# Two moves in a four-layer graph network kernel: layer 0's factors ahead of x, and the last block's third product around its last sums

## The chip, the cores and the metric

The kernel runs on one core of one Trainium2 chip, all in float32. The metric is the device time of one execution in microseconds (us). Three runs of the kernel before took 2646.83, 2647.34 and 2647.69 us; the median, 2647.34 us, is what a changed kernel is held against.

## The reference

The input x holds 128 graphs of 64 nodes with 512 features. Each of four layers normalizes x, takes the positive part, runs a graph layer on it and adds the result to x:

```python
h = jnp.maximum(_layernorm(x, axis=-1), 0.0)
x = x + _L0_gnn_ref(h, adj, nodemask, L0_gnn_Wqk, L0_gnn_Wv)
```

Layer 0 computes, for each node, `w = -q . (adj @ (k * mask))` up to a scale, with `q = h @ Wq`, `k = h @ Wk`, and multiplies `softmax(w) * (h @ Wv)`. Because q and k only meet in a product, the kernel works with one folded matrix, Wq times the transpose of Wk, which it computes itself at the start. Layers 1 and 2 are attention layers with the adjacency as weight or mask; layer 3 is a graph attention layer with three powers of the transition matrix:

```python
for k in range(Wk.shape[0]):
    H = H + Xk @ Wk[k] + bk[k]
    Xk = jnp.einsum('bij,bjd->bid', transition, Xk)
return jax.nn.relu(H)
```

In the kernel this is reordered: y1 = h Wk1 and y2 = h Wk2 are formed first, then y1 + A y2, then y0 + A (y1 + A y2), where A is the transition matrix and y0 = h Wk0 plus the sum of the three bias rows.

## The kernel before

The 8192 tokens are cut into 32 blocks of 256 tokens (four graphs), each two tiles of 128. Layers 0 and 1 run for two blocks at a time, in the order 0, 0, 1, 1 (`steps`, L915); then layer 2 runs over all blocks, then layer 3. The result of layer 1 and of layer 2 is kept in device memory between the passes.

A product of a block with a 512 x 512 weight (class `Product`, L228) is computed with seven half-size products in place of eight. `sums` (L209) makes the four sums of the block's quarters S1 to S4 on POOL (GpSimd); `formed` (L85) makes the four sums of the weight's quarters. Each of the seven is two matmuls of 128 x 256 columns (L256 or L249). The products use two PSUM tiles of one bank each: ab holds the halves a and b, dc holds d and c. Product 1 starts a, 6 starts b, 5 starts c, 4 is d; later 2 is added to a, 7 to b and 3 to c. Between them `keep_ab` (L281) copies a to p1 and forms u2 = b + p1, and `keep_dc` (L288) copies c to p5. The four quarters of the result are a, c + u2, d + u3 and u3 + p5, with u3 = b + p1 after product 7.

`neighbour_sums` (L390) multiplies a block by the adjacency or transition weights of its four graphs: four matmuls of 64 x 64 x 512 (L397), written to `pa` in layer 0 and to `po` in layer 3.

**The start.** At L136 the program issues the load of block 0's x, of its adjacency and of the mask on SP's queue. Then come the two factors of layer 0 (L139): q on ACT's queue and k on SP's, each in four pieces of 256 KB. The value weight of layer 0 (L143) and small rows follow. At L947 to L952 the order is: `prepare(0)`, the normalization of block 0 (`norm`, L164: statistics L169 and L170, ve L172, reciprocal root on POOL L174, nmr L176, h on ACT L184); `transpose_weight` of q (L416, sixteen transposes and four copies back into the same tile, two on DVE and two on ACT); `turned(0)`, the transposes of h (L195); `transpose_weight` of k, two of whose PSUM tiles come from the pool of the products; `setup0` (L450), which computes the fold in sixteen matmuls (L440), copies each piece out on ACT and DVE (L444, L445) and forms the four sums of the folded weight on DVE; and the sums of the value weight on POOL (L952). Layer 1's set-up (`setup1`, L459) loads that layer's weights and bias rows and does nine dot products on DVE (L478); the first of them, d, needs only the two bias rows.

**The end.** For a block b, `layer3_tail` (L851) runs y0's products 1, 6, 5 and 4, then the denominators (den, L861) and the second sums (`po2`), whose result updates y1 on DVE (L872), then products 2, 7 and 3 (`late`) and their results with the bias row bs (L881 to L886). `layer3_end` (L889) runs the last sums (`po3`), scales them by r, adds y0, takes the positive part, adds x (L904) and stores. Of the last block, tile 0 is scaled and added in one DVE operation (L896), while tile 1 goes through ACT (L900) and POOL (L903); the two tiles are stored apart (L908).

**What sets the order.** The program text gives the dependencies and a priority. A scheduler of the framework puts the instructions into each engine's queue when the kernel is built, by times that it models, and adds the waits. `tc.issue_after(i)` holds an instruction behind instruction i in that order. [...]

Of the kernel before, what the change touches and what calls it, by code (L numbers as in the profile page):

```python
# [8 lines left out]
FP = mybir.dt.float32  # L9
# [4 lines left out]
P = 128  # L14
# [11 lines left out]
def kernel(ctx: ExitStack, tc: tile.TileContext, a: dict, out: bass.AP):  # L26
# [101 lines left out]
    def factor(ap, which: str, layer: int, queue):  # L128
# [4 lines left out]
            queue.dma_start(w[:, k, :], ap[k * P : (k + 1) * P, :])  # L133
        return w

    first = load_x(0, x_d[rows(0), :], 0), load_adjT(0, 0)  # L136
    mcol = const.tile([P, n_tok // P], FP, tag="mcol", name="mcol")
    nc.sync.dma_start(mcol, a["maskcol"])
    f0 = [  # L139
        factor(a["L0_Wqk"][:, i * D : (i + 1) * D], c, 0, queue)  # L140
        for i, (c, queue) in enumerate((("q", nc.scalar), ("k", nc.sync)))
    ]
    w0v = fetched("L0_Wv", 1, nc.sync)  # L143
    b2q, b2k = (column(n) for n in ("L2_bq", "L2_bk"))
    b1v = row("L1_bv")
# [270 lines left out]
    def transpose_weight(w, name: str, places=((ps_mm, "mm"),) * K, on_scalar=(1, 3)):  # L416

        pts = [
            pool.tile([P, K, P], FP, tag=tag, name=f"tw_{name}_{m}")
            for m, (pool, tag) in enumerate(places)  # L420
        ]
        for k in range(K):
            for m, pt in enumerate(pts):
                nc.tensor.transpose(pt[:, k, :], w[:, k, m * P : (m + 1) * P], ident)
        for m, pt in enumerate(pts):
            flat = pt.rearrange("p k i -> p (k i)")
            if m in on_scalar:
                nc.scalar.copy(w[:, m, :], flat)
            else:
                nc.vector.tensor_copy(w[:, m, :], flat)  # L430

    elsewhere = ((ps_tr, "tr"), (ps_sc, "sc")) * 2

    def folded(aT, bT, layer: int, place: int, amid=lambda: None):

        m = slot(place, f"fold{layer}")
        for i in range(K):
            pm = ps_mm.tile([P, D], FP, tag="mm", name=f"pf_{layer}_{i}")
            for k in range(K):
                nc.tensor.matmul(  # L440
                    pm, aT[:, k, i * P : (i + 1) * P], bT[:, k, :],
                    start=(k == 0), stop=(k == K - 1),
                )
            nc.scalar.copy(m[:, quarters[i // 2][0], i % 2, :], pm[:, :F])  # L444
            nc.vector.tensor_copy(m[:, quarters[i // 2][1], i % 2, :], pm[:, F:])  # L445
            if not i:
                amid()
        return m

    def setup0():  # L450
        m = folded(*f0, 0, 0)
        formed(m, nc.vector)

        msc = const.tile([P, n_tok // P], FP, tag="msc", name="msc")
        with tc.issue_after(behind_norm[0][1].ins):
            nc.vector.tensor_scalar(msc, mcol, -(float(D) ** -0.5), None, ALU.mult)
        return m, msc
# [393 lines left out]
    def layer3_tail(b: int, al, ops, y):  # L851


        p = Product(f"y0_{b}")
        p.first(ops, w3[0])
        p.second(ops, w3[0])
        yield
        den = [ps_tr.tile([P, 1], FP, tag="tr", name=f"den3_{b}_{t}") for t in range(TT)]
        for t in range(TT):
            for g in range(2):  # L860
                nc.tensor.matmul(  # L861
                    den[t][half[g ^ t]], al[half[g], t, :], ones_bd[half[g], g * N : g * N + 1],
                    start=True, stop=True,
                )
        po = [ps_sc.tile([P, D], FP, tag="sc", name=f"po2_{b}_{t}") for t in range(TT)]
        parts = neighbour_sums(po, al, [y[:, 1, t, :] for t in range(TT)])
        r = small.tile([P, TT], FP, tag="r1", name=f"r3_{b}")
        for t in range(TT):
            nc.vector.tensor_scalar(r[:, t : t + 1], den[t], 1e-12, None, ALU.add)
        nc.vector.reciprocal(r, r)  # L870
        for t, to, at in parts:
            nc.vector.scalar_tensor_tensor(  # L872
                y[to, 0, t, :], po[t][at], r[at, t : t + 1], y[to, 0, t, :], ALU.mult, ALU.add
            )
        bs = made3[2]
        y0 = big.tile([P, TT, D], FP, tag="v", name=f"y0_{b}")
        nc.gpsimd.tensor_tensor(p.u2, p.u2, bs[:, F:], ALU.add)
        nc.gpsimd.tensor_tensor(p.p5, p.p5, bs[:, F:], ALU.add)
        yield
        p.late(ops, w3[0])  # L880
        nc.vector.tensor_tensor(y0[:, 0, :F], p.a, bs[:, :F], ALU.add)  # L881
        nc.vector.tensor_tensor(p.u3, p.b, p.p1, ALU.add)  # L882
        nc.vector.tensor_tensor(y0[:, 1, :F], p.d, p.u3, ALU.add)
        nc.gpsimd.tensor_tensor(y0[:, 1, F:], p.u3, p.p5, ALU.add)
        kept = nc.vector.tensor_tensor(y0[:, 0, F:], p.c, p.u2, ALU.add)
        nc.gpsimd.tensor_tensor(y0[:, 1, :F], y0[:, 1, :F], bs[:, :F], ALU.add)  # L886
        yield r, y0, kept

    def layer3_end(b: int, x, al, y, r, y0):  # L889

        po = [ps_sc.tile([P, D], FP, tag="sc", name=f"po3_{b}_{t}") for t in range(TT)]
        tz = [med.tile([P, D], FP, tag="pT", name=f"tz_{b}_{t}", bufs=3) for t in range(TT)]
        to, last = tokens(out[rows(b), :]), b + 1 == n_blk
        for t, out_at, at in neighbour_sums(po, al, [y[:, 0, t, :] for t in range(TT)]):
            if last and not t:
                nc.vector.scalar_tensor_tensor(  # L896
                    tz[t], po[t], r[:, t : t + 1], y0[:, t, :], ALU.mult, ALU.add
                )
            else:
                nc.scalar.activation(tz[t][out_at], po[t][at], AF.Copy, scale=r[at, t : t + 1])  # L900
        for t in range(TT):
            if not last or t:
                nc.gpsimd.tensor_tensor(tz[t], tz[t], y0[:, t, :], ALU.add)  # L903
            nc.vector.scalar_tensor_tensor(  # L904
                x[:, t, :], tz[t], 0.0, x[:, t, :], ALU.max, ALU.add
            )
            if last:
                nc.sync.dma_start(to[:, t], x[:, t])  # L908
        if not last:
            nc.sync.dma_start(to, x)  # L910


    x1 = [tc.dram_tile([T, D], FP, name=f"x1_{b}") for b in range(n_blk)]
# [11 lines left out]
    def turned(i: int):  # L925
        layer, b = steps[i]
        normed[i] = normed[i], transposed(normed[i], f"{layer}_{b}")
# [16 lines left out]
        if b < n_blk:  # L944
            normed2[b] = transposed(normed2[b], f"2_{b}")

    prepare(0)  # L947
    transpose_weight(f0[0], "q0")
    turned(0)
    transpose_weight(f0[1], "k0", ((ps_sc, "sc"),) * 2 + ((ps_mm, "mm"),) * 2)  # L950
    m0, msc = setup0()
    formed(w0v, nc.gpsimd)  # L952
    loaded[1] = load_x(1, x_d[rows(1), :], 0), load_adjT(1, 0)
    setup = setup1()
    next(setup)
# [39 lines left out]
    def layer3_step(b: int, ahead: bool = True):  # L995

        nonlocal normed3
        x, al, ops = made_in.pop(0)  # L1000
        stages = layer3_in(b + 1, *normed3, made_in) if b + 1 < n_blk else iter(())

        def begin():
            nonlocal normed3
            if b + 2 < n_blk and ahead:
                normed3 = layer3_norm(b + 2, x2[b + 2])

        y = layer3_head(b, ops, [
            [begin], [ending.pop()], [lambda: next(stages, None), lambda: next(stages, None)]
        ])  # L1010
# [6 lines left out]
        ending.append(lambda: layer3_end(b, x, al, y, r, y0))  # L1017
        if b + 2 < n_blk:
# [142 lines left out]
```

## Time and profile before

| what | value |
|---|---|
| median of three runs | 2647.34 us |
| the profiled execution's own time | 2645.07 us |
| its span | 2643.3 us |
| TensorE (PE) busy | 2624.6 us, 99% |
| VectorE (DVE) busy | 1695.9 us, 64% |
| GpSimd (POOL) busy | 1292.8 us, 49% |
| ScalarE (ACT) busy | 950.4 us, 36% |
| mean transfer rate over the span | 49 GB/s |
| first transpose on PE | 5.13 us |
| first product of block 0 on PE | 28.79 us |
| last sums on PE start | 2635.43 us |

The profile is of one execution on the core. Times count from the start of the span. In a timeline, a row gives the start, the time from the first to the last instruction of a merged group, the engine, the line in the kernel, the operation, its output and inputs with their sizes, the number of instructions, and in brackets how long the engine stood idle before it and what released it. PEld is the loading of weights into PE, which runs beside the matmuls. SPq and ACTq rows are the issue of transfers. Names in the trace leave out numbers: p_y stands for p1 and p5, u_y for u2 and u3, ab_v and ab_g for the products of layer 0 with the value weight and the fold.

### The profile page before, as it was taken

What the parts mean: (1) busy time and instruction counts of PE and PEld (TensorE: products, weight loads), DVE (VectorE), ACT (ScalarE), POOL (GpSimd) and SP (SyncE); (2) the same over time, 40 slices, a digit from 0 to 9 for tenths busy, and PEclk for the clock granted to TensorE, in tenths of its full rate; (3) what the DMA queues carried; (4) which work ended last, traced back from release to release, by engine and by line L of the source; (5) the groups of instructions that cost most, each with busy time, mean ns of one, the idle gap of its engine ahead of it and who ended that gap; (6) DMA issues with size and microseconds to landing.
All of it is one profiled execution on the core that took longest, in us unless ns stands there. A gap on an engine that the chain in (4) does not pass through costs nothing.

```text
span 2643.3 us, 52749 instructions
## 1 busy us (share of the span) xinstructions
PE 2624.6 (99%) x20752; PEld 2250.6 (85%) x20752; DVE 1695.9 (64%) x4396; ACT 950.4 (36%) x2292; POOL 1292.8 (49%) x1585
## 2 busy tenths in 40 slices
PE   9999999999999999999999999999999999999998
PEld 5888888888888889999999999999877777777776
DVE  5676666666666676556556656656656666666665
ACT  3333343333333343333333333333333333333332
POOL 4443333333433335655655655655565555555554
PEclk9999999999999999999999999999999999999999
DMA  5111111111111122111111111111211111111110
GB/s 179 48 35 35 35 36 37 46 39 43 43 35 35 35 67 79 39 51 40 37 53 38 39 53 37 39 48 42 74 51 52 51 52 52 52 52 51 52 50 32
DMA packets 103200, 129.80 MB, mean 49 GB/s; under 512 B 40870, under 2 KB 50086, under 8 KB 102952
## 3 DMA queue, kind: packets, MB, share of 16 engines
q1 hardware_dynamic: 102376, 125.38, 14.3%
q8 instruction: 163, 2.67, 0.4%
q10 hardware_dynamic: 576, 1.05, 0.1%
q14 instruction: 85, 0.70, 0.1%
HBM read 76.07 MB, written 50.34 MB: 48 GB/s over the span
## 4 chain that ended last, share of the span: by engine, by line
PE 93%; DVE 2%; DMA 2%; POOL 1%; ACT 1%; issue 0%; SPq 0%; ACTq 0%; POOLq 0%; DVEq 0%
PE ab_v L256 12%; PE ab_y L256 11%; PE dc_v L256 9%; PE dc_y L256 8%; PE ab_g L249 4%; PE ab_k L249 4%; PE ab_g L256 4%; PE ab_q L249 4%; PE tr L195 4%; PE ab_o L256 4%; PE dc_g L249 3%; PE dc_g L256 3%; PE po L397 3%; PE dc_k L249 3%; PE dc_q L249 3%; PE dc_o L256 3%
## 5 line engine op out<-in xcount | busy, mean ns | idle before, releaser
L184 ACT ACTIVATE h<-x,nmr,rstd 128x512 f32<-128x512 f32 x256 | 194.4, 806 | 239.8 <-DVE nmr L176 239.8
L174 POOL TENSOR_TENSOR rstd<-ve,neghalf 128x2 f32<-128x2 f32 x128 | 89.6, 700 | 373.8 <-DVE ve L172 373.8
L169 DVE BATCH_NORM_STATS2 stats<-x 128x6 f32<-128x512 f32 x256 | 165.5, 677 | 92.8 <-DMA x<-x 86.7
L256 PE MATMUL ab_y<-L_Wk,hT 128*128 128x256 f32 x768 | 203.9, 388 | 0.1
L256 PE MATMUL ab_v<-L_Wv,hT 128*128 128x256 f32 x768 | 200.8, 384 | 0.4 <-ACT qk L328 0.4
L256 PE MATMUL dc_v<-L_Wv,S 128*128 128x256 f32 x768 | 197.3, 380 | 0.0
L256 PE MATMUL ab_y<-L_Wk,S 128*128 128x256 f32 x768 | 197.2, 379 | 0.0
L256 PE MATMUL ab_v<-L_Wv,S 128*128 128x256 f32 x768 | 197.2, 379 | 0.0
L256 PE MATMUL dc_y<-L_Wk,S 128*128 128x256 f32 x768 | 193.8, 381 | 3.2 <-DVE u_y L882 3.1
L256 PEld LDWEIGHTS ab_y<-L_Wk,hT 128*128 128x128 f32 x768 | 137.3, 190 | 67.5 <-issue 25.2
L256 PEld LDWEIGHTS dc_y<-L_Wk,S 128*128 128x128 f32 x768 | 144.8, 190 | 26.6 <-DVE u_y L882 7.0
L256 PEld LDWEIGHTS ab_v<-L_Wv,S 128*128 128x128 f32 x768 | 146.1, 190 | 19.7
L256 PEld LDWEIGHTS ab_y<-L_Wk,S 128*128 128x128 f32 x768 | 146.1, 190 | 19.7
L256 PEld LDWEIGHTS dc_v<-L_Wv,S 128*128 128x128 f32 x768 | 143.6, 190 | 18.7 <-issue 0.8
L903 POOL TENSOR_TENSOR tz<-tz,y 128x512 f32<-128x512 f32 x63 | 91.3, 1450 | 126.0 <-ACT tz L900 125.9
L256 PEld LDWEIGHTS ab_v<-L_Wv,hT 128*128 128x128 f32 x768 | 136.0, 190 | 16.0 <-ACT qk L328 0.7
L195 PE MATMUL tr<-ident,h 128*128 128x128 f32 x1024 | 133.9, 274 | 0.0
L195 PEld LDWEIGHTS tr<-ident,h 128*128 128x128 f32 x1024 | 118.4, 142 | 7.3
L221 POOL TENSOR_TENSOR S<-hT 128x256 f32<-128x256 f32 x128 | 100.4, 784 | 34.0 <-ACT hT L198 33.6
L224 POOL TENSOR_TENSOR S<-hT 128x256 f32<-128x256 f32 x128 | 107.9, 843 | 7.1 <-DVE hT L200 7.1
L904 DVE SCALAR_TENSOR_TENSOR x<-tz,x 128x512 f32<-128x512 f32 x64 | 44.3, 692 | 102.6 <-POOL tz L903 102.6
L311 POOL TENSOR_TENSOR gv<-u_g,p_g 128x256 f32<-128x256 f32 x32 | 23.3, 729 | 173.0 <-DVE u_g L308 173.0
(238 smaller groups left out, 6474.6 us busy)
## 6 DMA issues: line engine op xcount, KB each, us to landing
x<-x SPq DMA_DIRECT2D x128, 512.0 KB, 3.5
x<-in_x_dram SPq DMA_DIRECT2D x32, 512.0 KB, 3.5
out_dram<-x SPq DMA_DIRECT2D x31, 512.0 KB, 2.8
adjT<-in_adjT_dram SPq DMA_DIRECT2D x64, 64.0 KB, 1.9
adjq<-in_adj_dram SPq DMA_DIRECT2D x64, 64.0 KB, 2.3
L_Wk<-in_L_Wk_dram SPq DMA_DIRECT2D x16, 256.0 KB, 5.5
L_Wv<-in_L_Wv_dram SPq DMA_DIRECT2D x12, 256.0 KB, 4.9
q<-in_L_Wqk_dram ACTq DMA_DIRECT2D x4, 256.0 KB, 5.3
```

The lines of the kernel that those rows point to most:

```text
L169: nc.vector.bn_stats(stats[:, t, :], x[:, t, :])
L174: by_rows = nc.gpsimd.tensor_tensor(rstd, ve, neghalf, ALU.pow)
L184: nc.scalar.activation(h, x[:, t, :], AF.Relu, bias=nmr[:, t : t + 1], scale=rstd[:, t : t + 1])
L195: nc.tensor.transpose(pt[:, k, :], h[:, k * P : (k + 1) * P], ident)
L221: nc.gpsimd.tensor_tensor(S1, A21, A22, ALU.add)
L224: behind[0] = nc.gpsimd.tensor_tensor(S3, A11, A21, ALU.subtract)
L249: nc.tensor.matmul(dst[:, m * P : (m + 1) * P], w[:, place, k, m * P : (m + 1) * P], left[:, k, :], start=key not in self.begun, stop=last ...
L256: nc.tensor.matmul(dst, left[:, k, :], w[:, place, k, :], start=key not in self.begun, stop=last and k == 1, skip_group_check=True,)
L311: nc.gpsimd.tensor_tensor(y[:, 1, F:], self.u3, self.p5, ALU.add)
L397: nc.tensor.matmul(ps[t][half[g ^ t]], e[half[g], t, :], us[t][half[g]], start=True, stop=True)
L903: nc.gpsimd.tensor_tensor(tz[t], tz[t], y0[:, t, :], ALU.add)
L904: nc.vector.scalar_tensor_tensor(x[:, t, :], tz[t], 0.0, x[:, t, :], ALU.max, ALU.add)
```

## The change

The factors q and k of layer 0 are issued ahead of block 0's x, adjacency and mask. Both are transposed ahead of all else; k's PSUM tiles all come from the pools of scores and transposes. `transpose_weight` now returns its last copies, and the normalization of block 0 is held behind those of k. The transposes of block 0's h are placed inside the fold, after its first piece. The sums of the value weight go from POOL to DVE, behind the nmr of block 0.

In the last block, products 5 and 4 of y0 follow the second sums; product 7 comes ahead of the last sums, and 3 and 2 behind them. Tile 0's half of y0 starts as the bias row, and a and c are added to its scaled sum at the very end. The other blocks are unchanged.

```diff
+    f0 = [
+        factor(a["L0_Wqk"][:, i * D : (i + 1) * D], c, 0, queue)
+        for i, (c, queue) in enumerate((("q", nc.scalar), ("k", nc.sync)))
+    ]
     first = load_x(0, x_d[rows(0), :], 0), load_adjT(0, 0)
     mcol = const.tile([P, n_tok // P], FP, tag="mcol", name="mcol")
     nc.sync.dma_start(mcol, a["maskcol"])
-    f0 = [
-        factor(a["L0_Wqk"][:, i * D : (i + 1) * D], c, 0, queue)
-        for i, (c, queue) in enumerate((("q", nc.scalar), ("k", nc.sync)))
-    ]
...
     def setup0():
-        m = folded(*f0, 0, 0)
+        m = folded(*f0, 0, 0, lambda: turned(0))
         formed(m, nc.vector)
...
-    prepare(0)
     transpose_weight(f0[0], "q0")
-    turned(0)
-    transpose_weight(f0[1], "k0", ((ps_sc, "sc"),) * 2 + ((ps_mm, "mm"),) * 2)
+    taken = transpose_weight(f0[1], "k0", ((ps_sc, "sc"),) * 2 + ((ps_tr, "tr"),) * 2)
+    with tc.issue_after(taken["vector"].ins), tc.issue_after(taken["scalar"].ins):
+        prepare(0)
     m0, msc = setup0()
-    formed(w0v, nc.gpsimd)
+    with tc.issue_after(behind_norm[0][1].ins):
+        formed(w0v, nc.vector)
...
         p = Product(f"y0_{b}")
+        last = b + 1 == n_blk
         p.first(ops, w3[0])
-        p.second(ops, w3[0])
+        if not last:
+            p.second(ops, w3[0])
...
-        nc.gpsimd.tensor_tensor(p.u2, p.u2, bs[:, F:], ALU.add)
+        if last:
+            p.second(ops, w3[0])
+        else:
+            nc.gpsimd.tensor_tensor(p.u2, p.u2, bs[:, F:], ALU.add)
         nc.gpsimd.tensor_tensor(p.p5, p.p5, bs[:, F:], ALU.add)
         yield
+        if last:
+            p.add(7, ops, w3[0])
+            nc.gpsimd.tensor_copy(y0[:, 0, :F], bs[:, :F])
+            nc.gpsimd.tensor_tensor(y0[:, 0, F:], p.u2, bs[:, F:], ALU.add)
+            nc.vector.tensor_tensor(p.u3, p.b, p.p1, ALU.add)
+            nc.gpsimd.tensor_tensor(y0[:, 1, F:], p.u3, p.p5, ALU.add)
+            nc.gpsimd.tensor_tensor(p.u3, p.u3, bs[:, :F], ALU.add)
+            nc.vector.tensor_tensor(y0[:, 1, :F], p.d, p.u3, ALU.add)
+            yield r, y0, p
+            return
...
+    def layer3_last(b: int, x, al, y, r, y0, ops, p):
+        po = [ps_sc.tile([P, D], FP, tag="sc", name=f"po3_{b}_{t}") for t in range(TT)]
+        tz = [med.tile([P, D], FP, tag="pT", name=f"tz_{b}_{t}", bufs=3) for t in range(TT)]
+        to = tokens(out[rows(b), :])
+        parts = neighbour_sums(po, al, [y[:, 0, t, :] for t in range(TT)])
+        p.add(3, ops, w3[0])
+        p.add(2, ops, w3[0])
+        nc.vector.scalar_tensor_tensor(
+            tz[0], po[0], r[:, :1], y0[:, 0, :], ALU.mult, ALU.add
+        )
+        for t, out_at, at in parts[1:]:
+            nc.scalar.activation(tz[t][out_at], po[t][at], AF.Copy, scale=r[at, t : t + 1])
+        nc.gpsimd.tensor_tensor(tz[1], tz[1], y0[:, 1, :], ALU.add)
+        nc.vector.tensor_tensor(tz[0][:, F:], p.c, tz[0][:, F:], ALU.add)
+        nc.vector.tensor_tensor(tz[0][:, :F], p.a, tz[0][:, :F], ALU.add)
+        for t in range(TT):
+            nc.vector.scalar_tensor_tensor(
+                x[:, t, :], tz[t], 0.0, x[:, t, :], ALU.max, ALU.add
+            )
+            nc.sync.dma_start(to[:, t], x[:, t])
```

In `layer3_step` the last block's end is `layer3_last`. The line of d + u3 in the changed kernel, in the last block, is L895.

More of the change, by code (lines that the diff above doesn't have):

```diff
@@ L134, in factor @@
         return w
-    first = load_x(0, x_d[rows(0), :], 0), load_adjT(0, 0)
-    mcol = const.tile([P, n_tok // P], FP, tag="mcol", name="mcol")
-    nc.sync.dma_start(mcol, a["maskcol"])
     f0 = [
@@ L142 @@
     ]
+    first = load_x(0, x_d[rows(0), :], 0), load_adjT(0, 0)
+    mcol = const.tile([P, n_tok // P], FP, tag="mcol", name="mcol")
+    nc.sync.dma_start(mcol, a["maskcol"])
     w0v = fetched("L0_Wv", 1, nc.sync)
@@ L424, in transpose_weight @@
                 nc.tensor.transpose(pt[:, k, :], w[:, k, m * P : (m + 1) * P], ident)
+        last = {}
         for m, pt in enumerate(pts):
@@ L427, in transpose_weight @@
             if m in on_scalar:
-                nc.scalar.copy(w[:, m, :], flat)
+                last["scalar"] = nc.scalar.copy(w[:, m, :], flat)
             else:
-                nc.vector.tensor_copy(w[:, m, :], flat)
+                last["vector"] = nc.vector.tensor_copy(w[:, m, :], flat)
+        return last
     elsewhere = ((ps_tr, "tr"), (ps_sc, "sc")) * 2
@@ L892, in layer3_end @@
         tz = [med.tile([P, D], FP, tag="pT", name=f"tz_{b}_{t}", bufs=3) for t in range(TT)]
-        to, last = tokens(out[rows(b), :]), b + 1 == n_blk
         for t, out_at, at in neighbour_sums(po, al, [y[:, 0, t, :] for t in range(TT)]):
[L895 to L900, printed above, removed]
+            nc.scalar.activation(tz[t][out_at], po[t][at], AF.Copy, scale=r[at, t : t + 1])
         for t in range(TT):
-            if not last or t:
-                nc.gpsimd.tensor_tensor(tz[t], tz[t], y0[:, t, :], ALU.add)
+            nc.gpsimd.tensor_tensor(tz[t], tz[t], y0[:, t, :], ALU.add)
             nc.vector.scalar_tensor_tensor(
@@ L906, in layer3_end @@
             )
[L907 to L910, printed above, removed]
+        nc.sync.dma_start(tokens(out[rows(b), :]), x)
+    def layer3_last(b: int, x, al, y, r, y0, ops, p):
[9 more added lines that the diff above has]
+        for t, out_at, at in parts[1:]:
+            nc.scalar.activation(tz[t][out_at], po[t][at], AF.Copy, scale=r[at, t : t + 1])
+        nc.gpsimd.tensor_tensor(tz[1], tz[1], y0[:, 1, :], ALU.add)
[6 more added lines that the diff above has]
+            nc.sync.dma_start(to[:, t], x[:, t])
     x1 = [tc.dram_tile([T, D], FP, name=f"x1_{b}") for b in range(n_blk)]
@@ L1017, in layer3_step @@
         ending.append(lambda: layer3_end(b, x, al, y, r, y0))
+        if b + 1 == n_blk:
+            ending[0] = lambda: layer3_last(b, x, al, y, r, y0, ops, kept)
         if b + 2 < n_blk:
```

## The prediction

> **What bounds the kernel now.** I read the page first, then the chain of waits at the start, the timeline of VectorE at the start and the timeline of the end.
>
> ```profile
> span 2643.3 us, 52749 instructions
> PE 2624.6 (99%) x20752; PEld 2250.6 (85%) x20752; DVE 1695.9 (64%) x4396; ACT 950.4 (36%) x2292; POOL 1292.8 (49%) x1585
> PE   9999999999999999999999999999999999999998
> ```
>
> TensorE (PE) is busy in every slice, and 18.7 us of the span are not PE work (2643.3 - 2624.6). Most of them lie at the two ends: 5.1 us before the first transpose, 6.8 us after the last matmul. The built program has the same PE order as before except in the first 45 rows and the last 15, so what can move is the time at which block 0's first product starts (28.79 before) and the time from the last block's products to the end.
>
> The chain of waits through the start (start, duration, what):
>
> ```profile
> 2.25 6.46 DMA q<-in_L_Wqk_dram
> ...
> 8.76 1.11 PE tw_q L424 x4
> 9.87 1.29 PE tr L195 x8
> 11.17 1.75 PE tw_k L424 x16
> 12.91 1.00 PE pa L397 x2
> 13.91 13.95 PE pf L440 x32
> ```
>
> From the landing of q on, PE itself is the chain: transposes of q, of h, of k, one of the four first sums (pa), the fold (16 matmuls, 0.87 us each). Nobody else is late. VectorE (DVE) in that time:
>
> ```profile
> 12.62 1.29 DVE L430 COPY k<-tw_k 128x512 f32<-128x512 f32 x2 [1.17 <-PE tw_k L424]
> 15.90 1.29 DVE L169 BATCH_NORM_STATS2 stats<-x 128x6 f32<-128x512 f32 x2 [1.99 <-DMA x<-in_x_dram]
> ...
> 17.60 1.14 DVE L478 SCALAR_TENSOR_TENSOR bias<-b1qk 128x512 f32<-128x512 f32 x1 [0.33 <-DMA b1qk<-in_L_bk_dram]
> ...
> 21.86 1.22 DVE L176 SCALAR_TENSOR_TENSOR nmr<-mv,rstd 128x2 f32<-128x2 f32 x1 [2.51 <-POOL rstd L174]
> ...
> 28.29 0.42 DVE L445 COPY fold<-pf 128x256 f32<-128x256 f32 x1 [0.55 <-ACT fold L444]
> ```
>
> The rows at 15.90 and 17.60 are block 1's statistics and layer 1's bias dot. Each stood waiting for a load: x of block 1 landed at 15.90, the bias rows at 17.6. In the kernel before that costs nothing, since h of block 0 was made by 9.93. The end:
>
> ```profile
> 2635.43 1.09 PE L397 MATMUL po<-y,al 64*64 64x512 f32 x8
> 2636.79 0.75 DVE L896 SCALAR_TENSOR_TENSOR tz<-po,r,y 128x512 f32<-128x512 f32 x1
> 2638.13 1.26 POOL L903 TENSOR_TENSOR tz<-tz,y 128x512 f32<-128x512 f32 x1 [0.75 <-ACT tz L900]
> 2639.42 0.69 DVE L904 SCALAR_TENSOR_TENSOR x<-tz,x 128x512 f32<-128x512 f32 x1 [1.15 <-POOL tz L903]
> 2640.14 0.34 SPq L908 DMA_DIRECT2D out_dram<-x  x1
> ```
>
> All products are done when the last sums (po) start; behind them lie ACT, POOL (GpSimd), DVE and the store, 3.2 us from the last DVE end (2640.11) to 2643.3.
>
> [...] block 1's second aggregate, free since 17.2, ran at 18.67, after the dot. [...] eight q transposes took 2.01 us (0.23 apart), sixteen k transposes 1.91 us (0.11 apart); the change came near 10.4, though the clock record reads 1.00 throughout. Nothing here shows a fall back. [...] from 4 us on they move 334 to 406 GB/s in each microsecond, whichever queue issues. [...] the DVE copy at 28.29 waits for ACT's copy of the other half of its tile.
>
> **The start, part by part.** Loads: k goes ahead of x on SP, and q, k are eight transfers of 0.26 MB. [...] x, issued at 0.74 before, goes out when q's first piece lands (5.0). That costs nothing: q and k are 2.1 MB, x ends at 2.62 MB, and the windows reach that by 9.6 (landing near 10.2), while its statistics stand behind the k copies on DVE (till about 13). The mask and adjT follow x; their user (am) has 20 us. For q I take 8.7 as before, since half the flow was the other queue's in both orders. The loads up to the bias rows are the same bytes in sum (5.15 MB), so block 1's x and the bias rows land as before: 15.9 and 17.6, give or take 0.4.
>
> PE: tw_k follows tw_q at 9.87. Some 2.5 of 16 transposes at 0.23 and 13.5 at 0.11 make 2.0 us, to 11.9; the fold then waits for the first k copy, which pa covered before: copy 12.62 to 13.27 against tw_k's end 12.91 gives 0.45. Fold at 12.4 instead of 13.84. Six of its matmuls (5.2 us) bring PE to 17.6, where h's eight transposes now stand.
>
> Is h there? The built order on DVE is: k copies, block 0's statistics of tile 0, **block 1's statistics**, block 0's second aggregate, ve, block 1's aggregates, **the bias dot**, and only then nmr of block 0 (L176), from which ACT makes h. So nmr stands behind both loads. With the rows above: statistics of block 1 from 15.9 to 17.2, ve, rstd on POOL (0.71) done by 18.2; dot 17.6 to 18.7; nmr by 19.1; h on ACT two times 0.76, 19.9 and 20.6; transposes 0.5 each, the second set done at 21.2. PE resumes the fold 2.5 us later than the 18.7 that an on-time h would give. Ten matmuls at 0.87 end at 29.9, the four pa together take 1.02 (as three did at 27.77): products start at 31.0 against 28.79, **+2.2 us**. All that was gained ahead (1.4 us) is swallowed, for the wait ends by a load, not by PE.
>
> The other moves here: layer 0's value weight is now formed on DVE, four operations of 0.70 to 1.69 (rows of L87), between nmr and 26.5; its first reader comes at 31.0. On POOL the four L1_Wv operations (1.27 each, 5.06 in all) now precede block 0's four S sums (0.7 to 1.2 each): done near 29.3, needed at 31.0. If that 1.7 us of cover goes, each microsecond costs one. ACT's copy of the second fold piece waits behind h of block 1 (near 27); four PSUM tiles hide it. Layer 1's loads of q and k wait for the fold's end, so they and their eight dots shift by the same 2.2 us. One dot more stands ahead of u_g on DVE: its cover was 0.9 us (done 38.35, PE there at 39.26), a dot takes 1.05: **+0.15**. The load of ab goes behind those of q and k on SP: nothing waits for it. Start in all: +2.35.
>
> **The end, in before's clock.** Products 1 and 6 as before till 2629.68. Then den and the second sums at 2629.8, products 5, 4 and 7 (three times 0.86), last sums at 2633.6 instead of 2635.43; DVE's three updates (2.28) end at 2633.3, so they are in time. Behind the sums stand products 2 and 3, in the order: half of 2, both halves of 3, half of 2. Product 3 writes the bank whose other half (d) L895 reads, and the built program has it wait for DVE there. L895 needs: product 7's result, 1.06 us after its start at 2632.7 (as the copy at 2629.88 came after 2628.82) = 2633.76; u3 on DVE 0.42; two POOL additions of 0.72 (spaced 0.68) to 2635.6; then 0.42, done 2636.1. PE, at that point by 2635.1, stands 1 us. Remaining halves, 3 x 0.43, last result 2637.65; one addition 0.42; **two** x updates of 0.69, since the built DVE order puts tile 1's behind that addition and ahead of tile 0's: 2639.45 against 2640.11. The store costs the same 3.2. **-0.65 us.** Bounds: POOL's addition took 1.21 where DVE ran beside it (2594.17), twice that makes +0.3; without the wait of product 3 PE would finish at 2636.4, tile 1's POOL addition at 2637.4, x at 2638.75: -1.35.
>
> Sum: +2.35 - 0.65 = +1.7. The profiled run took 2645.07 (span 2643.3 and 1.8 around it), 2.27 less than the median 2647.34; so 2646.8 profiled, **2649.0** timed. About 0.2%, or 5.3 us, is what a measurement of this kernel can tell from no change: this is "the same".
>
> **Rivals.** (A) h comes in time: the loads of block 1 and the bias land by 15.3, or wait less than the rows say. Then fold, 12.4 + 13.95 + 1.04 + 1.02 = 28.4, products -0.4, end -0.65: **2646.3**. For it: the moves do shorten PE's own work. Against it: the order on DVE and the landing at 17.6. (B) Product 3's wait costs nothing: 2649.0 - 0.7 = **2648.3**. Against it: the two POOL additions that precede it. (C) Slower: the idle 2.3 us at 17.6 sends PE back to half clock. The start needed 5.3 us of activity (5.13 to 10.4) to leave it; that much cold work loses 2.65 us: **2651.7**; it decides for "slower" from a cold spell of 7.3 us (3.65 lost, past 2652.6), and the ten matmuls left bound it at 8.7 lost. [...]
>
> **How the numbers follow.** Forecast (2648.5 to 2649.8) 0.6, A 0.17, B 0.12, C 0.11. The range 2646.2 to 2651.4 takes in A, B and the bounds of the end, and leaves out most of C. Faster than 2642.05 would need more than both ends hold (1.4 + 1.35): 0.01. Slower than 2652.6: the long end of C, 0.04. The same: 0.95.
>
> **What would show it.** In the changed profile PE stands idle near 17.6 for about 2.3 us, released by ACT's h, that by nmr, that by the dot and the bias load; products start near 31.0. At the end PE stands about 1 us before product 3, released by DVE L895, and tile 0's x is the last DVE instruction. Products starting before 28.8 would refute the start; no wait at product 3 the end.

## The result, and the profile after

The changed kernel took 2649.41 us (median of 21 runs, 2646.94 to 2653.48), the kernel before 2645.77 us in the runs beside it (21 runs, 2643.82 to 2648.78). The ratio is 1.0013, with a 95% interval of 1.0007 to 1.0019: by this ratio 3.4 us longer, between 1.9 and 5.0 (the two medians differ by 3.6). The profiled execution took 2648.56 us with a span of 2646.7, against 2645.07 and 2643.3. That is inside the 0.2% that I had called the same, but it is a small loss and not nothing: the interval excludes 1.

The head of the page of the changed kernel, the rows that answer to those shown of before:

```profile
span 2646.7 us, 52751 instructions
...
PE 2626.1 (99%) x20752; PEld 2249.3 (85%) x20752; DVE 1696.7 (64%) x4400; ACT 951.0 (36%) x2292; POOL 1288.7 (49%) x1582
...
PE   8999999999999999999999999999999999999999
```

The slices show the loss in one digit: the first slice, that is the first 66 us, fell from 9 to 8. PE's busy time even grew, by 1.5 us, with the same 20752 matmuls; some of them ran slower (which ones, is shown below). The chain of waits through the start of the changed kernel:

```profile
8.56 4.86 DMA L_Wv<-in_L_Wv_dram
...
14.80 4.63 DMA L_Wv<-in_L_Wv_dram
19.46 0.82 ACT h L184
20.32 1.82 PE tr L195 x8
22.15 9.68 PE pf L442 x20
```

PE is no longer the chain up to 20 us. Loads are, then h, then the transposes of h. (The chain names a load of the value weight as what released h, where the second profile of the same kernel, below, names nmr; VectorE's timeline tells what h really waited for.) The timeline of VectorE in the changed kernel, with block 0's reciprocal root on POOL put in at its time:

```profile
16.73 0.69 DVE L169 BATCH_NORM_STATS2 stats<-x 128x6 f32<-128x512 f32 x1 [2.41 <-DMA x<-in_x_dram]
...
18.00 0.15 DVE L172 TENSOR_SCALAR ve<-mv 128x2 f32<-128x2 f32 x1
18.31 0.71 POOL L174 TENSOR_TENSOR rstd<-ve,neghalf 128x2 f32<-128x2 f32 x1 [16.85 <-DVE mv L170]
18.45 0.69 DVE L480 SCALAR_TENSOR_TENSOR bias<-b1qk 128x512 f32<-128x512 f32 x1 [0.15 <-DMA b1qk<-in_L_bk_dram]
...
19.07 0.35 DVE L176 SCALAR_TENSOR_TENSOR nmr<-mv,rstd 128x2 f32<-128x2 f32 x1
```

Block 0's nmr stands directly behind block 1's statistics and the bias dot, and both of these stood waiting for a load. That is the queue that the prediction read from the built order. Of the two loads, though, only the first decides. Block 0's own ve (18.00) stands behind block 1's statistics too, and the root on POOL that needs it ends at 19.02. (The bracket of its row names an aggregate that ended just as it started.) nmr started at 19.07, when VectorE had left the dot. With the old end, and with d + u3 first (both below), the root ended at 19.81 and 20.40 and nmr started 0.03 us later. In the changed kernel and in its second profile, nmr came 0.05 and 0.09 us after the root. So the bias dot cost at most 0.1 us there, and what set h was the landing of block 1's x. The end, all engines:

```profile
2637.06 1.09 PE L397 MATMUL po<-y,al 64*64 64x512 f32 x8
2637.12 0.73 POOL L885 TENSOR_TENSOR p_y<-p_y,bs 128x256 f32<-128x256 f32 x1 [2.11 <-ACT p_y L293]
...
2637.93 0.72 POOL L893 TENSOR_TENSOR y<-u_y,p_y 128x256 f32<-128x256 f32 x1
...
2638.73 0.72 POOL L894 TENSOR_TENSOR u_y<-u_y,bs 128x256 f32<-128x256 f32 x1
2639.49 0.42 DVE L895 TENSOR_TENSOR y<-dc_y,u_y 128x256 f32<-128x256 f32 x1 [0.48 <-POOL u_y L894]
2639.96 1.13 PE L256 MATMUL dc_y<-L_Wk,S 128*128 128x256 f32 x4 [1.19 <-DVE y L895]
...
2641.91 1.28 DVE L937 SCALAR_TENSOR_TENSOR x<-tz,x 128x512 f32<-128x512 f32 x2
```

PE stands 1.19 us at product 3, released by L895, which waits for POOL's L894. POOL has three additions in a row there, not two: L885, c's copy plus the bias row, comes first, because ACT made that copy only at 2636.68.

### The profile page after: what moved, and what is told of

Its sections match the earlier page's. It is cut to its first block, busy times and chain, and to the rows that moved or that the text cites. A ratio compares the mean times of both kernels' runs of the same rounds, so it can differ in the third digit from the quotient of the medians.

```text
span 2646.7 us, 52751 instructions
## 1 busy us (share of the span) xinstructions
PE 2626.1 (99%) x20752; PEld 2249.3 (85%) x20752; DVE 1696.7 (64%) x4400; ACT 951.0 (36%) x2292; POOL 1288.7 (49%) x1582
## 3 DMA queue, kind: packets, MB, share of 16 engines
q8 instruction: 163, 2.67, 0.4%
## 4 chain that ended last, share of the span: by engine, by line
PE 92%; DMA 3%; DVE 2%; POOL 1%; ACT 1%; issue 0%; SPq 0%; ACTq 0%; DVEq 0%; POOLq 0%
PE ab_v L256 12%; PE ab_y L256 11%; PE dc_v L256 9%; PE dc_y L256 8%; PE ab_g L249 4%; PE ab_k L249 4%; PE ab_q L249 4%; PE ab_g L256 4%; PE tr L195 4%; PE ab_o L256 4%; PE dc_g L249 3%; PE po L397 3%; PE dc_g L256 3%; PE dc_k L249 3%; PE dc_q L249 3%; PE dc_o L256 3%
## 5 line engine op out<-in xcount | busy, mean ns | idle before, releaser
L221 POOL TENSOR_TENSOR S<-hT 128x256 f32<-128x256 f32 x128 | 100.4, 784 | 34.3 <-ACT hT L198 34.2
```

What stands on the lines that cost most here:

```text
L221: nc.gpsimd.tensor_tensor(S1, A21, A22, ALU.add)
```

## The experiments

**The numbers of all runs.** "First product" is the start of block 0's first product, "sm_w" of the first graph sum (the point from which block 0's products are behind), "end" the time from product 1 of the last block's y0 to the end of the last x. These three are from one profiled execution each. The ratio is to the kernel before on the same chip, with its 95% interval.

| kernel | ratio | first product | sm_w | end | span |
|---|---|---|---|---|---|
| before (shown profile) | | 28.79 | 46.3 | 12.16 | 2643.3 |
| before, again | 1.0001 [0.9993, 1.0009] | 30.12 | 47.6 | 12.15 | 2643.7 |
| changed (shown profile) | 1.0013 [1.0007, 1.0019] | 32.76 | 50.5 | 11.87 | 2646.7 |
| changed, again | 1.0013 [1.0006, 1.0019] | 33.18 | 51.4 | 11.87 | 2649.8 |
| new start, old end | 1.0014 [1.0007, 1.0021] | 31.99 | 49.7 | 12.16 | 2646.9 |
| old start, new end | 1.0002 [0.9994, 1.0010] | 29.13 | 46.6 | 11.87 | 2643.5 |
| changed, nmr ahead | 1.0016 [1.0009, 1.0022] | 30.04 | 49.9 | 11.87 | 2648.0 |
| changed, filler in the wait | 1.0013 [1.0006, 1.0019] | 31.67 | 49.4 | 11.87 | 2645.7 |
| changed, transposes later | 1.0007 [0.9999, 1.0015] | 30.25 | 48.7 | 11.87 | 2647.1 |
| changed, d + u3 first | 1.0008 [1.0000, 1.0016] | 32.58 | 50.6 | 11.03 | 2646.4 |
| old start, d + u3 first | 0.9998 [0.9990, 1.0007] | 30.01 | 48.1 | 11.32 | 2644.8 |
| changed, dots behind u_g | 1.0022 [1.0013, 1.0032] | 30.07 | 56.7 | 11.68 | 2649.8 |
| transposes later, d + u3 first | 1.0003 [0.9995, 1.0011] | 30.16 | 48.9 | 11.03 | 2644.6 |
| old start, tile 1 on VectorE | 0.9993 [0.9985, 1.0001] | 30.02 | 47.7 | 10.62 | 2641.8 |

Single spans don't compare well. From sm_w to product 1 of the last block the like programs (all rows but "dots behind u_g") took 2579.9 to 2583.0 us; the changed kernel itself took 2580.8 once and 2583.0 once. So I read the stages, and use the ratios for sums.

**One half at a time.** The theory: all of the loss lies at the start, and the end gains little or nothing. First the new start with the end of before (the end's hunks taken back):

```diff
         p = Product(f"y0_{b}")
-        last = b + 1 == n_blk
+        last = False
...
```

> Only the moves at the start, with the end of the kernel before. Theory: the whole loss is at the start (nmr of block 0 behind the loads of block 1 and of the bias rows on DVE, and PE's clock falling back in the wait), so first product at 32.8 us and 3.5 to 4.0 us more than before (ratio 1.0013 to 1.0015). Rival (the loss is at the end, through the wait of product 3): no more than 2 us over before.

Then the start of before with the new end (the order of the loads and the engine of the value weight's sums go back as well):

```diff
...
-    taken = transpose_weight(f0[1], "k0", ((ps_sc, "sc"),) * 2 + ((ps_tr, "tr"),) * 2)
-    with tc.issue_after(taken["vector"].ins), tc.issue_after(taken["scalar"].ins):
-        prepare(0)
+    turned(0)
+    transpose_weight(f0[1], "k0", ((ps_sc, "sc"),) * 2 + ((ps_mm, "mm"),) * 2)
...
```

> Only the moves at the end, with the start of the kernel before; first product at 28.8. Theory: the gain of the end is eaten by the wait of product 3 and by two stores on top of each other, so within 0.5 us of before. Rival: the end brings its full 0.65 or 1.35 us, or costs 1 us or more.

The new start alone gives 1.0014, as much as the whole change; the new end alone 1.0002, with 1 inside its interval, and its wait at product 3 is 1.19 us again. The loss is the start's.

**nmr ahead of block 1's work.** The theory: h waits for VectorE's queue. Block 1's norm and the first dot are held behind block 0's nmr, and nothing else is changed in the program text:

```diff
-        dots((d, bias[:, 0], 1))
+        with tc.issue_after(behind_norm[0][1].ins):
+            dots((d, bias[:, 0], 1))
...
+        if i == 1:
+            with tc.issue_after(behind_norm[0][1].ins):
+                normed[i] = norm(loaded[b][0], f"{layer}_{b}")
```

> The changed kernel, with block 1's normalization and the first bias dot held behind block 0's nmr. Theory: h of block 0 is there by 16.7, PE waits under 1 us and its clock does not fall back; first product at 29.2 instead of 32.8, so 3.5 us less than the changed kernel and within 0.6 us of before. Rival (the wait is for x of block 0 itself, or for PE's transposes): PE still waits 2 us or more for h, and no more than 1 us is won back.

Block 0's nmr came at 16.44 instead of 19.07. The wait for h shrank from 2.53 to 0.7 us, although the scheduler now put h's transposes earlier, behind four and five fold matmuls instead of six, and the first product came at 30.04. So the queue is what made h late. The edit moves the statistics and the dot together; that the statistics are what counts is read from the traces above. But the ratio stayed at 1.0016. The waits of PE in this kernel (what waited, for what, us in total, times, longest), and then its VectorE timeline:

```profile
PE ab_g L256 <- DVE u_g L286: 1.5, 1, 1.5
...
PE tr L195 <- ACT h L184: 0.7, 1, 0.7
```

```profile
29.62 0.16 DVE L176 SCALAR_TENSOR_TENSOR nmr<-mv,rstd 128x2 f32<-128x2 f32 x1 [5.85 <-POOL rstd L174]
...
34.23 1.05 DVE L480 SCALAR_TENSOR_TENSOR bias<-q,b1qk 128x512 f32<-128x512 f32 x1
...
42.34 0.42 DVE L286 TENSOR_TENSOR u_g<-ab_g,p_g 128x256 f32<-128x256 f32 x1
```

The gain was handed on. Block 1's nmr now stood 5.85 us for a root on POOL, behind four additions for layer 1's value weight; it came at 29.62, and its h stood on ACT ahead of the fold's last copies. So the fold was formed by 34.2, eight dots of layer 1 (34.23 to 42.34) followed in one row, and u_g stood behind them: PE waited 1.5 us for it (and 0.4 for u_v). sm_w was 49.9 again.

**A filler in the wait.** The clock record of the changed kernel reads 0.50 after the wait (22 to 24 us). Is the half clock the cost? Twenty transposes of the identity are put where PE stands, and they and h's transposes are held behind the sixth fold matmul:

```diff
...
+            for n in range(0 if t else filler):
+                nc.tensor.transpose(pt[:, n % K, :], ident, ident)
             for k in range(K):
                 nc.tensor.transpose(pt[:, k, :], h[:, k * P : (k + 1) * P], ident)
...
```

> The changed kernel with 20 transposes of the identity, whose result nobody reads, on PE in the wait for h. Nothing on any other engine changes its inputs. Theory (the idle lets the clock fall to half, which costs 1.5 to 1.7 us after it): the clock stays full, the ten matmuls of the fold behind the wait take 8.7 us instead of 9.7, the transposes of h 1.2 instead of 1.8, first product at 31.3 instead of 32.8. Rival (the slow matmuls have another cause, such as memory traffic): first product at 32.8 or later, and no gain.

The record stays at 1.00, the ten fold matmuls take 8.75 us instead of 9.68, and the first product comes at 31.67, near the 31.3 expected. But this trace does not show that the filler did it. Its k transposes took 3.62 us, and in the two profiles without a filler where they took as long (old end; d + u3 first) the clock did not fall either. The filler also ran a little past h: from the start of h on ACT to the next fold matmul took 2.42 us here, 2.06 and 2.07 in those two. The time does not follow: 2649.07 us, ratio 1.0013, as without the filler. The half clock costs 1.4 to 1.6 us where it comes, but it does not come in every execution, as the repeated runs below show, and the interval of the ratio is as wide as that cost. So this run leaves the share of the half clock in the loss open.

**The transposes of h one piece later.** Eight fold matmuls now stand ahead of them. The program text moves nothing else; in the built order, the copies of what they yield (hT) and POOL's sums S come later with them (S from 28.16 instead of 26.85):

```diff
-            if not i:
+            if i == at:
                 amid()
...
-        m = folded(*f0, 0, 0, lambda: turned(0))
+        m = folded(*f0, 0, 0, lambda: turned(0), 1)
```

> The changed kernel with the transposes of h one fold piece later (behind eight fold matmuls instead of four or six). Theory (PE only waits because the transposes stand where h is not yet there): the four more matmuls (3.5 us) cover the wait of 2.5 us, PE waits 0.3 us or less for h, the first product starts near 29.5 instead of 32.76, sm_w near 47 instead of 50.48, and the time falls by about 3 us to that of the kernel before (ratio 1.000, give or take 0.0006). Rival (a later point sets the time, as where nmr was put ahead: fold copies, eight dots, u_g on VectorE): the first product is early as well, but PE then waits 1 to 2 us for u_g or for the sums S, sm_w stays near 50, and the ratio stays near 1.0014.

PE's waits in this kernel:

```profile
PE ab_g L256 <- DVE u_g L286: 0.7, 1, 0.7
...
PE tr L195 <- ACT h L184: 0.4, 1, 0.4
```

Both theories had a part. The wait for h is down to 0.4 and the first product at 30.25, within 0.3 of the three kernels with the old start whose k transposes took 2.55 to 2.79 us (30.01 to 30.12). But 0.7 us of it are lost again at u_g, and sm_w is at 48.7, 0.6 to 1.0 later than theirs (47.6 to 48.1). The ratio halves, to 1.0007; its interval holds both 1 and 1.0014, so the traces carry this verdict, not the timing.

**d + u3 first.** The bias row is added afterwards, on POOL, so that product 3 no longer waits for POOL by way of L895:

```diff
+            nc.vector.tensor_tensor(y0[:, 1, :F], p.d, p.u3, ALU.add)
             nc.gpsimd.tensor_tensor(y0[:, 1, F:], p.u3, p.p5, ALU.add)
-            nc.gpsimd.tensor_tensor(p.u3, p.u3, bs[:, :F], ALU.add)
-            nc.vector.tensor_tensor(y0[:, 1, :F], p.d, p.u3, ALU.add)
+            nc.gpsimd.tensor_tensor(y0[:, 1, :F], y0[:, 1, :F], bs[:, :F], ALU.add)
```

> The changed kernel, with d + u3 put on VectorE right behind u3, ahead of the bias row, which GpSimd adds afterwards. Theory (product 3 stands behind two GpSimd additions by way of L895): PE's wait of 1.2 us at product 3 is gone, the products behind the last sums end about 1.2 us earlier, the last x about 0.7 us earlier, and the time falls by 0.7 us at most, so 2648.7 and a ratio near 1.0010. Rival (the end is set by tile 1's way over ScalarE and GpSimd): PE's wait is gone all the same, but tile 1's addition on GpSimd comes last, and from product 1's start to the last x it stays at 11.9 us, the time unchanged.

The end of this kernel:

```profile
2638.14 0.42 DVE L893 TENSOR_TENSOR y<-dc_y,u_y 128x256 f32<-128x256 f32 x1
...
2638.62 1.13 PE L256 MATMUL dc_y<-L_Wk,S 128*128 128x256 f32 x4
...
2640.20 1.26 POOL L933 TENSOR_TENSOR tz<-tz,y 128x512 f32<-128x512 f32 x1 [0.42 <-ACT tz L932]
2640.65 0.42 DVE L935 TENSOR_TENSOR tz<-ab_y,tz 128x256 f32<-128x256 f32 x1 [0.44 <-PE ab_y L256]
2641.50 1.29 DVE L937 SCALAR_TENSOR_TENSOR x<-tz,x 128x512 f32<-128x512 f32 x2 [0.43 <-POOL tz L933]
```

Product 3 has no bracket: the wait is gone. The end is 0.84 us shorter (11.03 against 11.87), so the first theory holds; and the rival is right about what is late next, since the x update stands 0.43 us for POOL's addition of tile 1. The same edit on the old start:

> The start of the kernel before with the new end, d + u3 first on VectorE. Theory: the start costs nothing and the end gains what the wait for L895 had swallowed: 0.7 us below the kernel before, 2645.1, ratio 0.9997; from product 1 of the last block to the last x 11.2 us against 12.16. Rival (end set by tile 1's way, or by the two stores that lie together): 11.9 us or more, ratio 1.0000 to 1.0004.

The end is 11.32 us against 12.16, the ratio 0.9998. A gain of 0.8 us is 0.03%, below what the timing can tell. That it is 11.32 here and 11.03 with the new start lies in POOL's addition of tile 1, which started 0.72 us after its last work in place of 0.42, though ACT's part was as early; the profile names no cause for it.

**The dots behind u_g.** If the chain over the copies, the forming and the eight dots gives back what nmr ahead had won, it can be cut: on top of nmr ahead, the dots are held behind u_g, and the sums of layer 1's value weight are on VectorE, so that block 1's root on POOL isn't behind them.

```diff
...
+        with tc.issue_after(kept_ab["g0_0"].ins):
+            dots(*((u[:, k : k + 1], x, 1) for k, x in enumerate(columns(qT))))
+            dots(*((cc[:, k : k + 1], x, 0) for k, x in enumerate(columns(kT))))
...
-        formed(w1v, nc.gpsimd)
+        with tc.issue_after(behind_norm[1][1].ins):
+            formed(w1v, nc.vector)
```

> The changed kernel with block 0's nmr ahead of block 1's statistics and the first dot; the other eight dots held behind u_g of block 0; and the sums of layer 1's value weight on VectorE instead of GpSimd, so that block 1's rstd does not stand behind them. Theory (with nmr ahead, 3.5 us were given back by block 1's late h ahead of the fold's copies on ScalarE and by eight dots ahead of u_g): block 1's nmr comes near 25 instead of 29.6, the fold's copies follow their matmuls within 0.6 us, PE waits nowhere for u_g, sm_w comes near 47.3 instead of 49.93, and the time falls to 2646.5 (ratio 1.0003). Rival (the shift comes from elsewhere, such as the loads of layer 1, which wait for the fold's end): sm_w stays near 50, ratio 1.0014.

The chain was cut as expected: block 1's nmr at 24.88, u_g at 36.82, no wait for it among block 0's products up to 43.1. And then the kernel lost more than ever, 1.0022:

```profile
46.36 0.69 DVE L200 COPY hT<-tr 128x512 f32<-128x512 f32 x1
46.96 0.42 DVE L309 TENSOR_TENSOR u_g<-ab_g,p_g 128x256 f32<-128x256 f32 x1
```

```profile
PE tw_q L425 <- DVE u_g L309: 3.3, 1, 3.3
```

The last dots ran from 43.05 to 46.4, ahead of the late result of g, and the transposes of layer 1's factor had to wait 3.3 us for it, that is, for the reading of g's PSUM tile. The dots are some 8 us of VectorE work that must lie between the landing of layer 1's factors and the copies that write their transposes back over them. Holding them back only moves the collision. My expectation asked who stood in front of u_g, and not who would stand behind the dots.

**Both kernels once more.** Does the half clock belong to the changed program, and is 28.79 what the old start always does?

> The changed kernel once more, for a second profile. Theory (how early TensorE leaves half clock differs from execution to execution, and the fall back in the wait for h comes only in some): the wait for h is 2.0 to 2.6 us again; if the k transposes take more than 3 us, the clock record stays at 1.00 and the first product starts near 32.6; if they take 2.5 us or less, the record falls to 0.5 and the first product starts at 32 to 33 all the same. Rival (the half clock behind the wait belongs to this program): the record reads 0.5 after the wait again, the ten fold matmuls take over 9.3 us. Ratio 1.0013 either way.

> The kernel before once more. Theory (the shown profile of before had an early full clock): the k transposes take 1.9 to 3 us, the first product starts between 28.8 and 30.1, sm_w between 46.3 and 48.1, and the difference to the changed kernel's start is then 2.5 rather than 4.0 us. Rival (28.79 is what the program always does): 28.6 to 29.0 again. Ratio 1.0000 give or take 0.0008, which is what the timing can tell.

PE in the second profile of the changed kernel, and then in the second of before:

```profile
9.88 2.45 PE L424 MATMUL tw_k<-ident,k 128*128 128x128 f32 x16
12.78 5.42 PE L442 MATMUL pf<-k,q 128*128 128x512 f32 x12 [0.46 <-DVE k L431]
20.73 1.82 PE L195 MATMUL tr<-ident,h 128*128 128x128 f32 x8 [2.53 <-ACT h L184]
22.35 9.88 PE L442 MATMUL pf<-k,q 128*128 128x512 f32 x20
```

```profile
11.58 2.67 PE L424 MATMUL tw_k<-ident,k 128*128 128x128 f32 x16
...
30.12 1.13 PE L256 MATMUL dc_v<-L_Wv,S 128*128 128x256 f32 x4
```

The shown profile of before had fast k transposes (1.91 us; 2.67 in the second) and the earliest landing of block 1's x (15.90; 17.16 in the second). Five profiles of the old start have their first product at 28.8 to 30.1, mean 29.6, and sm_w at 47.3 in the mean. Four of the new start as it stands (shown, again, old end, d + u3 first) have 32.0 to 33.2, mean 32.6, and 50.5. So the new start costs 3.0 us at the first product and 3.3 at sm_w. The half clock came in two of these four, just those in which the k transposes took 2.4 to 2.5 us; where they took 3.62 us, PE waited 1.83 and 2.52 us and the record stayed at 1.00. The second of these, with d + u3 first:

```profile
9.99 3.62 PE L424 MATMUL tw_k<-ident,k 128*128 128x128 f32 x16
...
21.68 1.36 PE L195 MATMUL tr<-ident,h 128*128 128x128 f32 x8 [2.52 <-ACT h L184]
22.88 8.75 PE L442 MATMUL pf<-k,q 128*128 128x512 f32 x20
```

The stages of the shown profile by windows (window, its sum, busy time of PE, PEld, DVE, ACT, POOL with instructions, granted PE clock, DMA share, GB/s):

```profile
20.60:20.80 0.20, 0.20 (x4) 0.14 (x2) 0.20 (x1) 0.20 (x1) 0.20 (x1) 0.94 1.07 389
20.80:22.00 1.20, 1.20 (x7) 0.97 (x6) 1.20 (x2) 0.18 (x1) 1.09 (x2) 0.50 1.08 358
22.00:24.00 2.00, 2.00 (x4) 0.95 (x4) 2.00 (x4) 0.58 (x1) 2.00 (x3) 0.50 1.11 323
24.00:24.20 0.20, 0.20 (x1) 0.00 (x0) 0.20 (x1) 0.00 (x0) 0.20 (x1) 0.52 1.18 282
24.20:25.00 0.80, 0.80 (x3) 0.38 (x2) 0.80 (x2) 0.00 (x0) 0.80 (x1) 1.00 1.27 192
```

The clock falls near 20.78 (0.94 over 0.2 us is 0.02 us at half) and returns near 24.19, 3.41 us later; in the second profile it falls near 21.21 and returns near 24.62, again 3.41. The fall comes 0.46 and 0.48 us after PE has begun again (20.32 and 20.73). Why a wait of 2.53 us was followed by it in two executions and one of 2.52 us in a third was not, these four profiles do not show.

**Both mends together.** Transposes later and d + u3 first:

> The changed kernel with both mends: transposes of h behind eight fold matmuls, and d + u3 first on VectorE. Theory (the two are independent): the start costs 0.3 to 0.6 us against the kernel before, the end gains 0.8, so 0.3 us below before, ratio 0.9999; no wait at product 3, 0.4 us or less for h. Rival (something else in the changed start sets the time, such as u_g behind the eight dots or later waits): ratio 1.0007 as with the first mend alone.

The two are independent: first product 30.16, end 11.03. The ratio is 1.0003, which can't be told from 1, nor from the first mend alone. The start did not come down as far as expected: PE still waits 0.6 us for h, where 0.4 at most was expected, and then 1.0 us for u_g behind the dots. sm_w at 48.9 is 1.6 later than the mean of the old start (47.3), where 0.3 to 0.6 was expected.

**Tile 1 on VectorE.** The profile with d + u3 first names POOL's addition of tile 1 as the last wait. On the old start, it goes to VectorE and tile 1 is stored first:

```diff
-        nc.gpsimd.tensor_tensor(tz[1], tz[1], y0[:, 1, :], ALU.add)
         nc.vector.tensor_tensor(tz[0][:, F:], p.c, tz[0][:, F:], ALU.add)
-        nc.vector.tensor_tensor(tz[0][:, :F], p.a, tz[0][:, :F], ALU.add)
-        for t in range(TT):
+        nc.vector.tensor_tensor(tz[1], tz[1], y0[:, 1, :], ALU.add)
+        for t in (1, 0):
+            if not t:
+                nc.vector.tensor_tensor(tz[0][:, :F], p.a, tz[0][:, :F], ALU.add)
```

> The start of before, the new end with d + u3 first, and tile 1's sum with y0 on VectorE in place of GpSimd, tile 1 stored first. Theory (GpSimd's addition of 1.26 us on tile 1, behind its two others, sets the end once the wait is gone): from product 1 of the last block to the last x 10.6 us against 11.3 with GpSimd and 12.16 before, the span some 0.7 us shorter than that with GpSimd for the same start; time 1 to 1.5 us below before, ratio 0.9995. Rival (the store alone sets what is left): last x earlier, but the span from it to the end grows by as much.

```profile
2635.68 0.42 DVE L931 TENSOR_TENSOR tz<-dc_y,tz 128x256 f32<-128x256 f32 x1 [0.34 <-PE dc_y L256]
2636.06 0.69 DVE L932 TENSOR_TENSOR tz<-tz,y 128x512 f32<-128x512 f32 x1
2636.67 0.42 DVE L935 TENSOR_TENSOR tz<-ab_y,tz 128x256 f32<-128x256 f32 x1
2637.00 1.28 DVE L936 SCALAR_TENSOR_TENSOR x<-tz,x 128x512 f32<-128x512 f32 x2
```

These rows of its end have no idle time after the first: VectorE is the end's chain now, and the end is 10.62 us, 1.54 less than before, as expected. From the last x to the end of the span it took 3.52 us, against 3.19 before and 3.26 with POOL's addition, so some 0.3 us of the gain may have gone back at the store, as the rival says; profiles with the same spacing of stores spread as much. The median is 2644.45 us against 2646.25, ratio 0.9993 with an interval of 0.9985 to 1.0001. It has the lowest median of all, and its end is shorter in the trace; that it is faster than the kernel before is not settled by the timing.

## Why the prediction was right, and where not

The kind of result was right (a small loss at the start that the end doesn't repay), and 2649.0 lies near the measured 2649.41. But the sum was not: I had +1.7 us, measured were +3.4 (1.9 to 5.0). The totals agree because I added my sum to 2647.34, the median of three runs, while 21 runs have 2645.77. That is luck: a base 1.6 us too high met a sum 1.7 us too low.

- **The fold's start, 12.4 after a wait of 0.45.** The shown profile has 12.38 and 0.46. Right (though the two figures that the wait was taken from, 13.27 and 12.91, differ by 0.36 only), but only for k transposes that ended as early as here (11.92); other executions had 12.8 to 13.75, and there the old start is late as well.
- **nmr behind block 1's statistics and the bias dot, PE idle 2.3 to 2.5 us at the transposes of h.** Right: 2.53, 2.53, 1.83 and 2.52 us in four profiles. The dot, however, was not the last link: block 0's root on POOL ended within 0.1 us of it or after it, so the chain is block 1's x, ve, root, nmr. The size is in part luck: x landed 0.8 us later than assumed (16.73), while the dot took 0.69 us where I had 1.1. That it is the queue, and that the place of the transposes decides, is shown by the two runs that took the wait to 0.7 and 0.4 us.
- **"Block 1's x and the bias rows land as before: 15.9 and 17.6, give or take 0.4."** Too narrow. x landed at 16.7 to 18.1 with the new start (seven profiles that have its statistics in this place, mean 17.3) and at 15.9 to 17.3 with the old one (five, mean 16.6). One trace gave me the earliest landing of all, and I took it for the rule. Why the new start has it later in the mean is not shown. The 334 to 406 GB/s of the prediction are what all of the core's transfers moved together.
- **The idle time does not bring PE back to half clock (rival C, 0.11).** This step failed in part. That so short an idle stretch leaves the clock up was my estimate; nothing in the profile of before shows it. In two of four profiles the record read 0.50 after 2.53 us of idle time, in the other two it stayed at 1.00 after 1.83 and 2.52. Where it fell, the transposes of h took 1.82 us instead of 1.36, and the ten fold matmuls 9.68 and 9.88 instead of 8.75: 1.4 to 1.6 us, less than C's 2.65. In the same executions the k transposes were faster (2.42 and 2.45 us against 3.62), so their first product is only 0.7 us later in the mean than where the clock didn't fall (32.8 and 33.2 against 32.0 and 32.6).
- **One more dot ahead of u_g, +0.15.** 0.2 and 0.4 us in the two profiles of the changed kernel, 0.3 with d + u3 first. Right in kind. What I did not see is that this place is the second limit: when h comes in time, u_g becomes the wait (0.7 to 1.5 us). The rival A, "h comes in time, 2646.3", would have been too low for that reason.
- **The start in all, +2.35.** Measured 3.0 at the first product and 3.3 at sm_w, between means. The mis-sized terms are the landing and the clock, both of which move from execution to execution.
- **The end, -0.65.** Measured from product 1 to the last x: 11.87 against 12.16, so -0.29. The mechanism was right: product 3 waits for L895 behind POOL, 1.19 us where I had 1. The term that failed is "two POOL additions": there are three. L885 stood ahead of them, since product 5 moved behind the second sums and ACT's copy of c came only at 2636.68. L895 ended 8.59 us after product 1's start, where I had 8.15.
- **"The store costs the same 3.2."** From the last x to the end of the span it took 3.2 to 3.6 us in the eleven profiles whose two stores are issued 0.6 us apart (mean 3.5), and 3.2, 3.2 and 3.4 in the three with the old end (1.8 us apart). About 0.2 more in the mean, which takes most of what was left of the end's gain. But the old start with the new end has 3.2 as well, and the spread is as large as the difference, so it is not shown that the nearness of the two stores costs this.

Start +3.3 and end -0.1 (with the store) make +3.2, against +3.4 timed. What stays open: how often the half clock comes over all executions, and so what part of the 3.4 is its.

## What to carry to other kernels

When a step is moved behind other work of its engine, look at what each instruction ahead of it waits for: here block 1's statistics of 0.69 us stood 2.41 us for a load, with block 0's nmr behind them, and that wait swallowed the 1.46 us by which the fold had started earlier (12.38 against 13.84). A stall that is removed uncovers the next one (here u_g behind eight dots, then a PSUM tile read late), so follow the freed work to the engine where it must be done. One profile is one execution: where a start moves from execution to execution (block 1's x landed at 15.9 to 18.1, the k transposes took 1.91 to 3.62 us), take two profiles of each kernel before a difference of 1 or 2 us is explained.

## What the runs showed of the hardware that I had not expected

- After an idle stretch of 2.53 us the clock record of PE read 0.50, for 3.41 us, in both profiles of the changed kernel; after stretches of 1.83 us (old end) and 2.52 us (d + u3 first) it stayed at 1.00.
- In the first 10 to 13 us transposes came 0.23 us apart and then 0.11 (sixteen k transposes took 3.62 us with d + u3 first, where all were slow, and 1.91 in the shown profile of before, where none was), though the clock record reads 1.00 there. The record shows the later fall, but not the slow start.
- The middle of the program, 2580 us with the same instructions, differs by up to 3 us between executions.
